# Edge constants per edge in their original order, and a hand-ordered beginning, in a four-layer graph network kernel

## The chip, the cores and the metric

The kernel runs on one core of one Trainium2 chip. The metric is the device time of one execution in microseconds (us). The kernel before took 3554.51 us, the median of three runs from 3550.32 to 3556.36.

The engines are TensorE (PE, matrix products; PEld is its weight load), VectorE (DVE), ScalarE (ACT), GpSimd (POOL) and SyncE (SP, which here only issues transfers). Transfers are issued on SP's, ACT's and POOL's queues and are carried out by 16 DMA engines that all queues share.

## What is computed

The input `x` holds 128 graphs of 128 nodes with 256 features, `adj` is one 128 x 128 matrix for all, and there are 512 edges `src`, `dst`. Four layers follow, each as `x = layernorm(x + layer(x))`. Layer 0 is an attention over edges:

```
Xq, Xv = H @ W_lin.T, H @ W_val.T               # 4 heads of 64
e = einsum(leaky_relu(Xq[:, src] + Xq[:, dst], 0.2), a)
e = e + log(adj[src, dst] + 1e-8)
e_t = e.transpose(1, 0, 2)                      # edges first
m = segment_max(e_t, src);  ex = exp(e_t - m[src])
attn = ex / segment_sum(ex, src)[src]
Y = segment_sum(attn * Xv[:, dst], src)         # back to graph, node, feature
out = Y @ W_out.T
```

Layer 1 is three rounds of `adj^2 @ (h @ W)` with relu between them, layer 2 three products with the diagonal, the upper and the lower part of `adj`, and layer 3 a normalized adjacency product, two dense layers and two batch norms over all graphs.

## The kernel before

The graphs are worked in 32 quads of four. The main loop, `iteration(k)` for k from 0 to 32, is a software pipeline with the order of instructions written out by hand: it works layer 2 and the first half of layer 3 on quad k-1, the large products of layer 1 (`second`, line 325, and `third`, line 336) on quad k, the end of layer 0 and the start of layer 1 on quad k+1 (`stage_a`, `mix1`, `first`, `mix2`), the scores and the softmax of layer 0 on quad k+2, and the projection to `Xq` and `Xv` with its gather on quad k+3 (`values_in`, `values`, `gather`). PE runs through the list in order; so does every other engine and every queue. A second phase after the loop finishes layer 3.

One quad's path through layer 0 has these steps:

- `values_in` (lines 145 to 157) loads a quad of `x` to the single buffer `xg` on SP's queue, transposes it on PE (line 154) and copies it to `xt` (line 156). `values` (line 159 on) multiplies it with `wqv` (line 167), copies one half to `qt` on ACT (line 168) and the other to `xv` on DVE (line 169), and after the fourth graph writes `qt` to `qd` in DRAM (line 172).
- `gather` (line 174 on) fetches four tiles of 128 edges from `qd` with eight indirect transfers on POOL (line 180): by `src_idx`, then by `dst_idx`, which adds to what the first brought.
- `score` (line 184 on) does leaky relu, the product with `a` and a sum over 64 for each of the four tiles, three DVE instructions over 128 x 1024 (lines 190, 192 and 193).
- `softmax_parts` transposes the scores on PE (line 200), adds the edges' logarithms `log_row` (line 202) and does maximum and sum by segment as scans along the edges, which are sorted by source (lines 205, 208, 214 and 216), with Exp on ACT (line 212). It is a generator; the caller steps it between other work.
- `attention` transposes back (line 226) and divides (lines 228 and 230). `scatter` writes four tiles to the table `attd` in DRAM (line 236), each after the one before it has landed, and loads the table as `ad` on SP's queue (line 239). `by_row` re-arranges it on ACT (line 246). `stage_a` then aggregates (line 258), projects (line 270) and normalizes.

Ahead of the loop (lines 431 to 596 for the set-up and the loads, 655 to 688 for filling the pipeline) stands a beginning whose order the framework's scheduler chooses. It does quad 0's projection, the edge set-up, the adjacency set-up (`wt_t`, `split_t`, `diag_bc`, `ahat_t`), the loads of all weights, and then fills the pipeline: layer 0 up to `mix2` of quad 0, quad 1 up to its scatter, quad 2 up to its gather. The first instruction of the loop on PE is line 325 of `second(0)`.

The edge set-up sorts the edges by source with comparisons of 128 x 512 (`rank`, `perm`), turns sources and destinations into sorted columns and, broadcast over 128 partitions, sorted rows (`ends_ps`, line 489), and computes each edge's constants in the sorted order: how often the pair occurs (`count`, line 517), whether it occurred earlier (`again`, `earlier`, line 520), and `adj[src, dst]` through two one-hot products (lines 540 and 544). The logarithm is kept as a row of 16 x 512.

Of the kernel before, what the change touches and what calls it, by code (L numbers as in the profile page):

```python
# [17 lines left out]
LOG_EPS = 1e-8  # L18
# [6 lines left out]
def gnn_stack(ctx: ExitStack, tc: tile.TileContext, x, adj, w_qv_t, a, w_out_t, src, dst,  # L25
# [80 lines left out]
    with ExitStack() as phase:  # L106
# [14 lines left out]
        a_sb = cload([P, N], "adj", adj)  # L121
        xg0 = load_x(0, "xg", 1)
        wqv = cload([P, DC, 2 * D], "wqv", w_qv_t.rearrange("(c p) f -> p c f", p=P))
        a_bc = cload([P, D], "a_bc", bass.AP(tensor=a.tensor, offset=a.offset, ap=[[0, P], [1, D]]), nc.scalar)

# [7 lines left out]
        log_row = ctile([R, E], "log_row", pool=cst)  # L133
# [11 lines left out]
        def values_in(k, xg=None):  # L145

            s = quads[k]
            s.xts = []
            xg = load_x(k, "xg", 1) if xg is None else xg
            for j in range(0, QB, 2):  # L150
                pt = ps("pt").rearrange("p (b c n) -> p b c n", b=2, c=DC)
                for t in range(2):
                    for c in range(DC):
                        nc.tensor.transpose(pt[:, t, c, :], xg[:, j + t, c * P:(c + 1) * P], ident)  # L154
                xt = ws.tile([P, 2, DC, P], F32, tag="xt", name="xt")
                nc.vector.tensor_copy(xt, pt)  # L156
                s.xts.append(xt)

        def values(k, i):

            s = quads[k]
# [7 lines left out]
            nc.vector.tensor_copy(s.xv[:, i, :], pq[:, D:])  # L169
# [4 lines left out]
        def gather(k):  # L174

            s = quads[k]
            s.z = [ws.tile([P, QB * D], F32, tag="zs", name=f"zs{k}_{c}", bufs=NE) for c in range(NE)]
            for idx, op in ((src_idx, ALU.bypass), (dst_idx, ALU.add)):
                for c in range(NE):
                    nc.gpsimd.indirect_dma_start(out=s.z[c], out_offset=None, in_=s.qd,  # L180
                                                 in_offset=bass.IndirectOffsetOnAxis(ap=idx[:, c:c + 1], axis=0),
                                                 compute_op=op)

        def score(k, c):
# [8 lines left out]
            nc.vector.reduce_sum(s.es[:, c, :], z.rearrange("p (r d) -> p r d", d=DH), axis=AX.X)  # L193

        def softmax_parts(k):
# [5 lines left out]
            e = wk.tile([R, E], F32, tag="e", name="e", bufs=1)  # L201
            nc.vector.tensor_add(e, log_row, pe[:R, :])
            yield
            f = wk.tile([R, E], F32, tag="f", name="f", bufs=1)
            nc.vector.tensor_tensor_scan(f, reset_f, e, initial=0.0, op0=ALU.add, op1=ALU.max)
# [5 lines left out]
            nc.vector.tensor_sub(e, e, m)  # L211
# [217 lines left out]


        values_in(0, xg0)
        for i in range(QB):
            values(0, i)
        with tc.tile_pool(name="set", bufs=1) as sp:
            src_col = cload([P, NE], "src_col", src.rearrange("(c p) -> p c", p=P), nc.scalar, I32, sp)
            dst_col = cload([P, NE], "dst_col", dst.rearrange("(c p) -> p c", p=P), nc.scalar, I32, sp)
            src_row = cload([P, E], "src_row", bass.AP(tensor=src.tensor, offset=src.offset, ap=[[0, P], [1, E]]),
                            nc.scalar, I32, sp)
            ones = ctile([P, P], "ones", pool=sp)
            nc.vector.memset(ones, 1.0)  # L440
            zero = ctile([P, N * R], "zero", pool=sp)
            nc.gpsimd.memset(zero, 0.0)
            for ad in att_dram:
                nc.scalar.dma_start(ad[:N * N, :].rearrange("(t s) r -> t (s r)", s=N), zero)


            pos = ctile([P, E], "pos", pool=sp)
            nc.gpsimd.iota(pos, pattern=[[1, E]], base=0, channel_multiplier=0,
                           allow_small_or_imprecise_dtypes=True)
            pos_col = ctile([P, NE], "pos_col", pool=sp)  # L450
            nc.gpsimd.iota(pos_col, pattern=[[P, NE]], base=0, channel_multiplier=1,
                           allow_small_or_imprecise_dtypes=True)
            ends = ctile([P, 2, NE], "ends", pool=sp)
            nc.vector.tensor_copy(ends[:, 0, :], src_col)
            nc.vector.tensor_copy(ends[:, 1, :], dst_col)
            key_row = ctile([P, E], "key_row", pool=sp)
            nc.vector.tensor_copy(key_row, src_row)
            nc.vector.scalar_tensor_tensor(key_row, key_row, float(E), pos, op0=ALU.mult, op1=ALU.add)
            key_col = ctile([P, NE], "key_col", pool=sp)
            nc.vector.scalar_tensor_tensor(key_col, ends[:, 0, :], float(E), pos_col, op0=ALU.mult, op1=ALU.add)  # L460

            less = ctile([P, NE, E], "less", pool=sp)
            rank = ctile([P, NE], "rank", pool=sp)
            perm = ctile([P, NE, E], "perm", pool=sp)
            bcast = ctile([P, 2, NE, P], "bcast", pool=sp)
            for c in range(NE):
                nc.vector.tensor_scalar(less[:, c, :], key_row, key_col[:, c:c + 1], None, op0=ALU.is_lt)
            nc.vector.reduce_sum(rank, less, axis=AX.X)
            for c in range(NE):
                nc.vector.tensor_scalar(perm[:, c, :], pos, rank[:, c:c + 1], None, op0=ALU.is_equal)  # L470
                for t in range(2):
                    nc.vector.tensor_copy(bcast[:, t, c, :], ends[:, t, c:c + 1].to_broadcast([P, P]))


            pc = ps("pcol")[:, :NE * 2].rearrange("p (c t) -> p c t", t=2)
            for c in range(NE):
                for i in range(NE):
                    nc.tensor.matmul(pc[:, c, :], perm[:, i, c * P:(c + 1) * P], ends[:, :, i],
                                     start=(i == 0), stop=(i == NE - 1))
            cols = ctile([P, NE, 2], "cols", pool=sp)  # L480
            nc.vector.tensor_copy(cols, pc)
            nc.vector.tensor_copy(src_idx, cols[:, :, 0])
            nc.vector.tensor_copy(dst_idx, cols[:, :, 1])

            ends_row = ctile([P, 2, E], "ends_row", pool=sp)
            for t in range(2):
                pr = ps("ends_ps")
                for c in range(NE):
                    nc.tensor.matmul(pr, bcast[:, t, c, :], perm[:, c, :], start=(c == 0), stop=(c == NE - 1))
                nc.vector.tensor_copy(ends_row[:, t, :], pr)  # L490


            pair_row = ctile([P, E], "pair_row", pool=sp)
            nc.vector.scalar_tensor_tensor(pair_row, ends_row[:, 1, :], float(N), ends_row[:, 0, :],
                                           op0=ALU.mult, op1=ALU.add)
            pair_col = ctile([P, NE], "pair_col", pool=sp)
# [103 lines left out]
        def iteration(k):  # L600
            a, c, b, e, g = k - 1, k, k + 1, k + 2, k + 3
            has_a, has_c, has_b, has_e, has_g = a >= 0, c < NQ, b < NQ, e < NQ, g < NQ
            if has_b:
                quads[b].xr = load_x(b, "xr", 3, wk)
# [200 lines left out]
```

## Time and profile before

| | |
|---|---|
| median of three runs | 3554.51 us |
| the profiled execution's own time | 3562.3 us |
| its span, from the first instruction to the last | 3560.1 us |
| PE busy | 3370.1 us, 95% of the span |
| DVE busy | 1801.2 us, 51% |
| ACT busy | 1004.9 us, 28% |
| POOL busy | 542.1 us, 15% |
| mean DMA rate | 98 GB/s |

The profile is of one execution, and its times are for comparing parts with each other. A page of it shows the busy share of each engine in 40 slices of 89 us as digits in tenths. A row of a windows table gives, for a stretch, the busy time of each engine with the number of its instructions, PE's granted clock, the DMA engines' busy share and the rate in GB/s. A row of waits names an instruction, what released it, the idle time in total, how often, and the longest. A row of the timeline gives start, duration, engine, line, operation and tiles.

### The profile page before, as it was taken

The numbers are of one execution on the slowest core, as the hardware profiler recorded it, in microseconds if no ns is written. First come the engines' busy times: TensorE is split into PE (matmuls) and PEld (weight loads), VectorE is DVE, ScalarE is ACT, GpSimd is POOL, SyncE is SP. The second block draws the span as 40 slices with busy tenths as digits, with TensorE's granted clock in tenths as the row PEclk, the third lists the DMA queues.
The fourth block names the chain that finished last, engine by engine and source line by source line (L and its number), as shares of the span: only waits on it lengthen the run. The fifth ranks groups of instructions, "written<-read, shape, count | busy, mean of one in ns | idle before, by whom it ended". The sixth has DMA issues, their size and how long they took to land.

```text
span 3560.1 us, 32948 instructions
## 1 busy us (share of the span) xinstructions
PE 3370.1 (95%) x12618; PEld 2146.1 (60%) x12618; DVE 1801.2 (51%) x3645; ACT 1004.9 (28%) x1733; POOL 542.1 (15%) x460
## 2 busy tenths in 40 slices
PE   5599999999999999999999999999999999989963
PEld 2366666666666666666666666666666666654442
DVE  6544455545545445544455555545445543223379
ACT  1122222222222222222222222222222222224452
POOL 2211111111111111111111111111111110000000
PEclk7799999999999999999999999999999999999975
DMA  6433333333222333333333333222333330025447
GB/s 190 124 83 89 90 95 95 85 87 93 80 76 73 89 95 95 95 95 90 88 95 95 89 84 95 81 77 74 85 95 95 95 89 36 18 95 183 154 137 223
DMA packets 127741, 347.72 MB, mean 98 GB/s; under 512 B 14433, under 2 KB 68577, under 8 KB 115041
## 3 DMA queue, kind: packets, MB, share of 16 engines
q0 software_dynamic: 40960, 135.29, 15.9%
q1 hardware_dynamic: 65168, 190.53, 15.0%
q10 hardware_dynamic: 21456, 19.81, 1.7%
q8 instruction: 99, 1.62, 0.2%
q14 instruction: 58, 0.47, 0.0%
HBM read 258.55 MB, written 87.03 MB: 97 GB/s over the span
## 4 chain that ended last, share of the span: by engine, by line
PE 88%; DVE 6%; DMA 2%; issue 1%; ACT 1%; POOL 0%; DVEq 0%; POOLq 0%; ACTq 0%; SPq 0%
PE ph L325 25%; PE p L336 13%; PE po L384 9%; PE po L739 6%; PE ph L423 6%; PE ph L305 6%; PE pq L167 6%; PE pm L315 3%; PE pm L370 3%; PE po L270 3%; PE py L258 2%; PE pa L409 2%; PE pm L291 2%; PE po L347 2%; DVE x3l L98 1%
## 5 line engine op out<-in xcount | busy, mean ns | idle before, releaser
L325 PE MATMUL ph<-m,w 128*128 128x512 f32 x2048 | 885.9, 593 | 2.7 <-DVE m L316 2.7
L325 PEld LDWEIGHTS ph<-m,w 128*128 128x128 f32 x2048 | 389.6, 190 | 480.1 <-issue 475.6
L336 PE MATMUL p<-w,h 128*128 128x256 f32 x2048 | 450.4, 381 | 0.0
L336 PEld LDWEIGHTS p<-w,h 128*128 128x128 f32 x2048 | 386.6, 190 | 52.6 <-issue 0.5
L180 POOL DMA_INDIRECT zs<-qd,src_idx x128 | 126.7, 989 | 1846.2 <-DVE f L214 1676.1
L384 PE MATMUL po<-l2w,ms 128*128 128x256 f32 x1536 | 347.5, 379 | 1.2 <-DVE ms L376 1.2
L328 ACT ACTIVATE h<-ph 128x512 f32<-128x512 f32 x256 | 153.2, 598 | 595.6 <-PE ph L325 595.6
L384 PEld LDWEIGHTS po<-l2w,ms 128*128 128x128 f32 x1536 | 284.3, 190 | 36.1 <-DVE ms L376 1.4
L305 PE MATMUL ph<-w,mx 128*128 128x512 f32 x512 | 236.3, 594 | 0.0
L167 PE MATMUL pq<-wqv,xt 128*128 128x512 f32 x512 | 232.0, 607 | 2.9 <-DVE xt L156 2.9
L739 PE MATMUL po<-zl,l3w 128*128 128x512 f32 x512 | 222.1, 597 | 10.4 <-ACT zl L734 10.4
L423 PE MATMUL ph<-ag,l3w 128*128 128x512 f32 x512 | 226.5, 595 | 0.4 <-ACT ag L412 0.4
L180 POOL DMA_INDIRECT zs<-qd,dst_idx x128 | 200.4, 1566 | 117.8 <-DMA zs<-qd,src_idx 95.5
L349 DVE TENSOR_TENSOR xr<-xr,po 128x512 f32<-128x512 f32 x64 | 43.8, 684 | 340.5 <-PE po L347 340.5
L156 DVE COPY xt<-pt 128x512 f32<-128x512 f32 x64 | 41.4, 686 | 309.5 <-PE pt L154 309.5
L236 POOL DMA_INDIRECT attd<-at,att_idx x128 | 127.9, 999 | 439.9 <-DMA attd<-at,att_idx 282.7
L90 ACT ACTIVATE ln_sd<-ln_mv,eps 128x2 f32<-128x2 f32 x256 | 75.8, 296 | 379.2 <-DVE ln_mv L85 374.1
L739 PEld LDWEIGHTS po<-zl,l3w 128*128 128x128 f32 x512 | 98.0, 192 | 134.5 <-issue 111.1
L190 DVE SCALAR_TENSOR_TENSOR zs<-zs 128x1024 f32<-128x1024 f32 x128 | 155.7, 1217 | 33.1 <-DMA zs<-qd,dst_idx 33.1
L423 PEld LDWEIGHTS ph<-ag,l3w 128*128 128x128 f32 x512 | 97.4, 191 | 122.3 <-issue 113.0
L167 PEld LDWEIGHTS pq<-wqv,xt 128*128 128x128 f32 x512 | 97.4, 195 | 115.8 <-issue 111.4
L316 DVE COPY m<-pm 128x512 f32<-128x512 f32 x128 | 88.4, 692 | 153.8 <-PE pm L315 153.8
(173 smaller groups left out, 4237.8 us busy)
## 6 DMA issues: line engine op xcount, KB each, us to landing
ad<-attd SPq DMA_DIRECT2D x32, 1024.0 KB, 4.7
zd<-z SPq DMA_DIRECT2D x32, 1024.0 KB, 7.4
zl<-zd SPq DMA_DIRECT2D x32, 1024.0 KB, 4.7
xg<-in_x_dram SPq DMA_DIRECT2D x32, 512.0 KB, 4.2
qd<-qt SPq DMA_DIRECT2D x32, 512.0 KB, 2.6
xr<-in_x_dram SPq DMA_DIRECT2D x32, 512.0 KB, 5.7
x3d<-xr SPq DMA_DIRECT2D x32, 512.0 KB, 2.9
x3l<-x3d SPq DMA_DIRECT2D x32, 512.0 KB, 4.2
```

Of the source, the lines that this page charges most:

```text
L167: nc.tensor.matmul(pq, s.xts[i // 2][:, i % 2, c, :], wqv[:, c, :], start=(c == 0), stop=(c == DC - 1))
L180: nc.gpsimd.indirect_dma_start(out=s.z[c], out_offset=None, in_=s.qd, in_offset=bass.IndirectOffsetOnAxis(ap=idx[:, c:c + 1], axis=0), com ...
L190: nc.vector.scalar_tensor_tensor(z, z, SLOPE, z, op0=ALU.mult, op1=ALU.max)
L236: nc.gpsimd.indirect_dma_start(out=ad, out_offset=bass.IndirectOffsetOnAxis(ap=att_idx[:, c:c + 1], axis=0), in_=s.at[:, c, :], in_offset= ...
L270: nc.tensor.matmul(po[:, i % 2, :], yts[i][:, dc, :], wo[:, dc, :], start=(dc == 0), stop=(dc == DC - 1))
L305: nc.tensor.matmul(ph, s.mx[i // 2 * 2][:, i % 2, dc, :], w1_sb[:, dc, :], start=(dc == 0), stop=(dc == DC - 1))
L325: nc.tensor.matmul(ph, w2_sb[:, c, f * P:(f + 1) * P], s.m2[:, c].rearrange("p b n -> p (b n)"), start=(c == 0), stop=(c == K1 - 1))
L328: nc.scalar.activation(h.rearrange("p b n -> p (b n)"), ph, AF.Relu)
L336: nc.tensor.matmul(p3[:, t * D:(t + 1) * D], s.h2[f][:, j + t, :], w3_sb[:, f, :], start=(f == 0), stop=(f == K2 - 1))
L384: nc.tensor.matmul(po[:, i % 2, :], mss[i][:, t, dc, :], l2w[:, t, dc, :], start=(n3 == 0), stop=(n3 == 3 * DC - 1))
L423: nc.tensor.matmul(ph, l3w1[:, dc, c * P:(c + 1) * P], s.ag[:, dc, :], start=(dc == 0), stop=(dc == DC - 1))
L739: nc.tensor.matmul(po, w2t[:, c, o * P:(o + 1) * P], z[:, c, :], start=(c == 0), stop=(c == K3 - 1))
```

## The change

The edge constants are computed per edge in the original order, as columns of 128 x 4: the comparisons add up their own result with an accumulated output, `adj[src, dst]` is fetched with four indirect transfers of 4 bytes for each edge, and the finished constants are brought to the sorted order with the same permutation product that sorts the ends (`sorted_columns`, called twice). The logarithm becomes a column `log_col`, which `score` adds to the scores before they are transposed; the add of `log_row` in `softmax_parts` goes away, and its scan and its subtraction read the transposed scores from PSUM.

The whole beginning becomes a function `start()` inside the hand-ordered part. In it, copies of `values_in` and `values` for quads 0 to 2 are on ACT; quad 0's gather has an interleaved order; the weights, the zero fill of `attd` and quad 0's `xr` are issued on SP's queue after quad 1's `qd`; quad 1's gather uses other tiles (`z`, `xb`, `ag`), and its scores stand after quad 0's scatter; the adjacency set-up stands between quad 0's scatter and quad 1's scores; quad 0's `stage_a` stands ahead of the last score and the softmax of quad 1; and quad 3's `values_in` and `values` are done there, with iteration 0 leaving them out. In the loop the softmax steps stand after the second and fourth product of `values` rather than after the first three. The diff, cut to its core:

```diff
-        a_sb = cload([P, N], "adj", adj)
         xg0 = load_x(0, "xg", 1)
         wqv = cload([P, DC, 2 * D], "wqv", w_qv_t.rearrange("(c p) f -> p c f", p=P))
-        a_bc = cload([P, D], "a_bc", bass.AP(tensor=a.tensor, offset=a.offset, ap=[[0, P], [1, D]]), nc.scalar)
-
+        a_sb = cload([P, N], "adj", adj)
+        a_bc = ctile([P, D], "a_bc", pool=cst)
...
-        def values_in(k, xg=None):
+        def values_in(k, xg=None, copy=None):
...
-                nc.vector.tensor_copy(xt, pt)
+                copy(xt, pt)
...
-            nc.vector.tensor_copy(s.xv[:, i, :], pq[:, D:])
+            copy(s.xv[:, i, :], pq[:, D:])
...
+            s.z = z or [ws.tile([P, QB * D], F32, tag="zs", name=f"zs{k}_{c}", bufs=NE) for c in range(NE)]
+            jobs = [(t, c) for t in range(2) for c in range(NE)]
+            if k == 0:
+                jobs = [(0, 0), (0, 1), (1, 0), (0, 2), (1, 1), (0, 3), (1, 2), (1, 3)]
+            for t, c in jobs:
+                idx, op = ((src_idx, ALU.bypass), (dst_idx, ALU.add))[t]
+                nc.gpsimd.indirect_dma_start(out=s.z[c], out_offset=None, in_=s.qd,
+                                             in_offset=bass.IndirectOffsetOnAxis(ap=idx[:, c:c + 1], axis=0),
...
+            if c == NE - 1:
+                nc.vector.tensor_add(s.es, s.es, log_col.unsqueeze(2).to_broadcast([P, NE, R]))
...
-            e = wk.tile([R, E], F32, tag="e", name="e", bufs=1)
-            nc.vector.tensor_add(e, log_row, pe[:R, :])
-            yield
             f = wk.tile([R, E], F32, tag="f", name="f", bufs=1)
-            nc.vector.tensor_tensor_scan(f, reset_f, e, initial=0.0, op0=ALU.add, op1=ALU.max)
...
-            nc.vector.tensor_sub(e, e, m)
+            e = wk.tile([R, E], F32, tag="e", name="e", bufs=1)
+            nc.vector.tensor_sub(e, pe[:R, :], m)
...
-        values_in(0, xg0)
-        for i in range(QB):
-            values(0, i)
-        with tc.tile_pool(name="set", bufs=1) as sp:
...
-            for c in range(NE):
-                nc.vector.tensor_scalar(less[:, c, :], key_row, key_col[:, c:c + 1], None, op0=ALU.is_lt)
-            nc.vector.reduce_sum(rank, less, axis=AX.X)
...
-            for ad in att_dram:
-                nc.scalar.dma_start(ad[:N * N, :].rearrange("(t s) r -> t (s r)", s=N), zero)
...
-            ends_row = ctile([P, 2, E], "ends_row", pool=sp)
-            for t in range(2):
-                pr = ps("ends_ps")
-                for c in range(NE):
-                    nc.tensor.matmul(pr, bcast[:, t, c, :], perm[:, c, :], start=(c == 0), stop=(c == NE - 1))
-                nc.vector.tensor_copy(ends_row[:, t, :], pr)
...
-            count = ps("count")
-            for c in range(NE):
-                nc.tensor.matmul(count, ones, same[:, c, :], start=(c == 0), stop=(c == NE - 1))
-            earlier = ps("earlier")
-            for c in range(NE):
-                nc.tensor.matmul(earlier, ones, less[:, c, :], start=(c == 0), stop=(c == NE - 1))
...
-            pr = ps("adj_e")
-            nc.tensor.matmul(pr, a_sb, g_src, start=True, stop=True)
-            picked = ctile([P, E], "picked", pool=sp)
-            nc.vector.tensor_mul(picked, g_dst, pr)
-            pr = ps("adj_e2")
...
-        gather(0)
-        edges(0)
-        whole(1)
-        attention(0)
-        scatter(0)
-        gather(1)
-        edges(1)
-        attention(1)
-        whole(2)
...
+            first_one = k == 0
...
-            if has_g:
+            if has_g and not first_one:
                 values_in(g)
...
-                if has_g:
+                if has_g and not first_one:
                     values(g, i)
-                if i < 3:
+                if i in (1, 3):
                     next(steps, None)
...
+        def start():
+            cols_i = wk.tile([P, 2, NE], I32, tag="cols_i", name="cols_i", bufs=1)
+            rows_i = [scratch(f"row_i{t}", I32) for t in range(2)]
+            for t, ap in ((0, src), (1, dst)):
+                nc.scalar.dma_start(cols_i[:, t, :], ap.rearrange("(c p) -> p c", p=P))
+            for t, ap in ((0, src), (1, dst)):
+                nc.scalar.dma_start(rows_i[t], bass.AP(tensor=ap.tensor, offset=ap.offset, ap=[[0, P], [1, E]]))
+            nc.scalar.dma_start(a_bc, bass.AP(tensor=a.tensor, offset=a.offset, ap=[[0, P], [1, D]]))
...
+            less = scratch("less")
+            for c in range(NE):
+                nc.vector.tensor_scalar(less, key_row, key_col[:, c:c + 1], 0.0, op0=ALU.is_lt, op1=ALU.add,
+                                        accum_out=rank[:, c:c + 1])
+            perm = wk.tile([P, NE, E], F32, tag="m2", name="perm", bufs=1)
+            for c in range(NE):
+                nc.vector.tensor_scalar(perm[:, c, :], pos, rank[:, c:c + 1], None, op0=ALU.is_equal)
...
+            for c in range(NE):
+                nc.gpsimd.indirect_dma_start(out=picked[:, c:c + 1], out_offset=None,
+                                             in_=adj.rearrange("n (m o) -> (n m) o", o=1),
+                                             in_offset=bass.IndirectOffsetOnAxis(ap=adj_idx[:, c:c + 1], axis=0))
+            values_in(0, xg0, nc.scalar.copy)
+            for i in range(QB):
+                values(0, i, nc.scalar.copy)
+            pc = sorted_columns(0)
+            nc.vector.tensor_copy(src_idx, pc[:, :, 0])
+            nc.vector.tensor_copy(dst_idx, pc[:, :, 1])
+            gather(0)
+            pr = ps("src_row")
+            for c in range(NE):
+                nc.tensor.matmul(pr[:R, :], src_wide[:, c, :], perm[:, c, :], start=(c == 0), stop=(c == NE - 1))
+            src_row = scratch("src_row")
+            nc.scalar.copy(src_row[:R, :], pr[:R, :])
...
+            same = scratch("same")
+            for c in range(NE):
+                nc.vector.tensor_scalar(same, pair_row, pair_col[:, c:c + 1], 0.0, op0=ALU.is_equal, op1=ALU.add,
+                                        accum_out=count[:, c:c + 1])
+                nc.vector.scalar_tensor_tensor(same, pos, pos_col[:, c:c + 1], same, op0=ALU.is_lt, op1=ALU.mult,
+                                               accum_out=again[:, c:c + 1])
...
+            nc.vector.scalar_tensor_tensor(weight, picked, LOG_EPS, count, op0=ALU.add, op1=ALU.mult)
+            nc.scalar.activation(weight, weight, AF.Ln)
+            nc.vector.scalar_tensor_tensor(ends[:, 3, :], again, DROP, weight, op0=ALU.mult, op1=ALU.add)
...
+            values_in(1, copy=nc.scalar.copy)
+            pc = sorted_columns(2)
+            nc.vector.tensor_copy(att_idx, pc[:, :, 0])
+            nc.vector.tensor_copy(log_col, pc[:, :, 1])
+            for i in range(QB):
+                values(1, i, nc.scalar.copy)
...
+            nc.sync.dma_start(wo, w_out_t.rearrange("(c p) f -> p c f", p=P))
+            nc.sync.dma_start(w1_sb, w1.rearrange("(c p) f -> p c f", p=P))
+            for ad in att_dram:
+                nc.sync.dma_start(ad[:N * N, :].rearrange("(t s) r -> t (s r)", s=N), zero)
+            quads[0].xr = load_x(0, "xr", 3, wk)
+            nc.sync.dma_start(w2_sb, w2.rearrange("(c p) f -> p c f", p=P))
+            nc.sync.dma_start(w3_sb, w3.rearrange("(c p) f -> p c f", p=P))
+            nc.sync.dma_start(l2w, l2_w.rearrange("k (c p) f -> p k c f", p=P))
+            nc.sync.dma_start(bias, bass.AP(tensor=l2_bias.tensor, offset=l2_bias.offset, ap=[[0, P], [1, D]]))
+            nc.sync.dma_start(l3w1, l3_w1_t.rearrange("(c p) f -> p c f", p=P))
+            for c in range(NE):
+                score(0, c)
+            z2 = wk.tile([P, 2, QB * D], F32, tag="z", name="z_1", bufs=1)
+            gather(1, [z2[:, 0, :], z2[:, 1, :], wk.tile([P, QB * D], F32, tag="xb", name="xb_1", bufs=1),
+                       wk.tile([P, QB * D], F32, tag="ag", name="ag_1", bufs=1)])
+            xg2 = load_x(2, "xg", 1)
+            steps = softmax_parts(0)
+            for _ in range(2):
+                next(steps)
+            values_in(2, xg2, nc.scalar.copy)
+            next(steps)
+            values(2, 0, nc.scalar.copy)
+            values(2, 1, nc.scalar.copy)
+            for _ in steps:
+                pass
+            attention(0)
+            for i in (2, 3):
+                values(2, i, nc.scalar.copy)
+            xg3 = load_x(3, "xg", 1)
+            scatter(0)
+            gather(2)
...
+            for c in range(NE - 1):
+                score(1, c)
+            for j in range(QB):
+                by_row(0, j)
+            stage_a(0)
+            score(1, NE - 1)
+            values_in(3, xg3)
+            steps = softmax_parts(1)
+            for i in range(QB):
+                next(steps)
+                values(3, i)
+            for _ in steps:
+                pass
+            attention(1)
+            scatter(1)
+            mix1(0, 0)
+            mix1(0, 2)
+            first(0, 0)
+            for i in range(QB):
+                if i + 1 < QB:
+                    first(0, i + 1)
+                mix2(0, i)
...
         with tc.manual_schedule(engines=None):
+            start()
             for k in range(NQ + 1):
                 iteration(k)
```

## The prediction

> **What bounds the kernel now.** I read the slices of the page first.
>
> ```profile
> span 3560.1 us, 32948 instructions
> ...
> PE   5599999999999999999999999999999999989963
> ...
> PEclk7799999999999999999999999999999999999975
> ```
>
> TensorE (PE) is full from slice 3 on; only the first two slices of 89 us and the last three are not. The diff touches the first two. Stage by stage:
>
> ```profile
> core 0: us, PE busy (x) PEld busy (x) DVE busy (x) ACT busy (x) POOL busy (x), PEclk, DMA share, GB/s
> 0.00:162.77 162.77, 84.97 (x267) 47.74 (x267) 94.89 (x164) 22.57 (x37) 44.99 (x44) 0.74 0.60 172
> 162.77:300.00 137.23, 134.68 (x462) 80.33 (x463) 63.64 (x108) 37.82 (x64) 18.73 (x17) 0.98 0.22 60
> ...
> 1000.00:2000.00 1000.00, 998.04 (x3852) 647.57 (x3851) 507.50 (x947) 276.05 (x479) 167.95 (x140) 1.00 0.30 86
> ```
>
> Before 162.77 us, where the first L325 matmul (`second(0)`) starts, PE is idle for 162.77 - 84.97 = 77.8 us. In the loop it is idle 2 us in 1000. So the whole question is when `second(0)` starts, and what of iteration 0 is done ahead of it. The waits of that stretch name the holes:
>
> ```profile
> PE pe L200 <- DVE es L193: 46.1, 6, 33.0
> PE half_ps L586 <- DVE half L584: 8.2, 1, 8.2
> PE pt L154 <- DMA xg<-in_x_dram: 7.3, 1, 7.3
> ```
>
> The 33.0 us are quad 1's scores waiting for a gather that shared the DMA engines with weights, scatter and attention table. SyncE's (SP's) queue in the timeline shows when they were issued:
>
> ```profile
> 58.19 0.37 SPq L111 DMA_DIRECT2D wo<-in_w_out_t_dram  x1
> 58.61 1.53 SPq L111 DMA_DIRECT2D w<-in_w_dram  x3
> 60.18 4.31 SPq L111 DMA_DIRECT2D l2w<-in_l_w_dram  x1
> 64.52 2.05 SPq L111 DMA_DIRECT2D bias<-in_l_bias_dram  x1
> 66.61 0.82 SPq L111 DMA_DIRECT2D l3w<-in_l_w_t_dram  x1
> ...
> 76.47 0.38 SPq L118 DMA_DIRECT2D xg<-in_x_dram  x1
> ```
>
> The rates, in windows of 5 us (columns as above):
>
> ```profile
> 60.00:65.00 5.00, 0.48 (x2) 0.18 (x2) 5.00 (x6) 0.00 (x0) 0.00 (x0) 0.50 1.04 410
> ...
> 95.00:100.00 5.00, 0.00 (x0) 0.00 (x0) 0.00 (x0) 0.00 (x0) 4.09 (x4) 0.50 0.83 162
> ```
>
> Weights alone move 410 GB/s. Beside an accumulating gather all traffic together makes 162.
>
> **What the Trainium skill says.** "DMA: Bandwidth & Descriptors", Queues, rings and completion order: on each DMA engine the descriptors of one queue are consumed in ring order; so a small load behind 8 MB on SP's queue comes last. Same page, SWDGE vs HWDGE vs iDMA: an engine goes round-robin between GpSimd's (POOL's) queue and the others. The trace agrees: the 1 MB load of `ad`, issued at 96.25 beside the gather of quad 1, landed at 105.15, 8.9 us, where the median over the page is 4.7. "TensorE: Matmul & The Clock Gate", What's actually happening: an idle PE falls to half clock. The trace has 0.50 from 80 to 120 us.
>
> **The change, part by part.** Times are of the profiled execution (span 3560.1, its own time 3562.3); I apply the difference to the median 3554.5, 7.8 below it.
>
> (1) Set-up, removed: 16 matmuls of `ends_ps` (9.43 us), the `count` and `earlier` ones (9.1), `adj_e` (2.1): 20.6 us of PE, plus DVE's reduces of 2048 (2.29 + 2.27), four `less` products, the row forms. Added: 8 matmuls for `src_row` (4.7 by `ends_ps`), a second `pcol` set (4.66), four 4-byte gathers of `adj` at 1.25 us of POOL each, if a small one costs what a 4 KB row does (hidden: adj_idx is there at about 9, so they end at 14, and `qd` lands only at 21; uncovered they would be 5 us). Accumulating forms of `less`, `same`, `again` aren't in the trace: at least the plain 0.42 and 0.66 us, at most double; I take 0.65 and 0.75. The spread is 12 x 0.4 = under 5 us, and most sits in (2), beside other work.
>
> (2) Quad 0 to gather(0). The copies of `xt` and `xv` go to ACT, which is idle. PE's first pq no longer waits for DVE (2.7): start 8.4 instead of 11.93, last `qt` at 18.4 instead of 21.9. The input of quad 1 is now behind this `qd` on SP's queue: issued at 18.8, there at 23.4 (4.6 to landing), and PE wants it after `src_row`, at 27.4: hidden. `pcol` 4.7, two casts: gather(0) starts at 23, not 26.9. Its new order makes dst 0 wait for src 0; z 0 lands by 39 at worst (dst issue to use was 7.5 at 145.5), and DVE is busy until then anyway: free.
>
> (3) Quad 1. DVE from 23: pair keys 0.85, four same/again pairs 6, small ones and Ln 1.6: 31.5. PE: second `pcol` to 36.3, then values(1) at 8.4 (as at 126.9): 44.7. Last `qt`, `qd` issued at 45. `pcol` waits at the head of PE's queue, but only values(1) is behind it.
>
> (4) Quad 0's scores: keep/reset to 38.5, then 4 x 3.74 (153.06 to 156.8) and the new 128x64 add at 0.2 (as L230): 53.7. Transposes, two scans, subtract: 57.5.
>
> (5) The new wait. SP's queue now holds `wo`, `w1`, the two 1 MB zero fills (until now on ACT's queue at the very start), `xr`, `w2`, `w3`, `l2w`, `bias`, `l3w` all behind `qd` of quad 1, and the `xg` of quad 2 behind them: 8.5 MB from 45. Behind this `xg` stand, on PE, pt and half of pq of quad 2 and then attention(0)'s pat; on ACT, two `xt` copies and then quad 0's Exp. So quad 0's softmax stops at 57.5 until quad 2's input is there. At the rate of the old weights (5.25 MB in 58.2 to 74.5, 322 GB/s) that is 26.5 us: 71. Gather(1) runs beside it: 2 MB at 386 GB/s (the window of 5 to 10 us) and 2 MB at 199 (35 to 40 us, accumulating) are some 15 us more of the same engines: 87 if all of it comes out of SP's share. I take 80; both ends go into the range.
>
> (6) From 80: transposes and copies 2.7, table load and Exp 1.9, two scans 2.5, pat, reciprocal, multiply 1.3: `at` at 88.4. Four scatters in a row, 10.3 (128.21 to the `ad` issue at 138.47): 98.7. `ad` load 4.7 to 8.9, I take 7, since gather(2) starts with it: 105.7; first by_row copy 106.8. The adjacency set-up, hidden before, now sits between attention(0) and score(1, 0 to 2): PE after the rest of pq at 92, its handshakes with DVE and a table load about 5, then 3 x 3.74: DVE is free at 108. So it costs 1 us here, on the path.
>
> (7) stage_a 10.5 (136.5 to 147.0): 118.5. score(1, 3) with the add 3.9: 122.4. Copies of `xt`, then softmax woven with values(3) 11.7 (192.7 to 204.3, less the dropped L202): 134.1. pat and mix1 to mix2: 0.8 and 17 (145.01 to 162.77 less 0.7 of wait): **second(0) at 152**, 10.8 earlier.
>
> (8) Iteration 0 drops values_in(3) and values(3). Before, from the end of second (192.0) to the first stage_a projection (204.84) 12.8 us passed. Now PE has only pe and py there, and waits for the softmax chain: 0.6 + two scans 2.4, 0.7, Exp 0.6, two scans 2.4, first `yt` 0.4, gaps 0.6: 7.7. Gain 5.1, not the 8 us of matmuls, since softmax is late next.
>
> (9) The loop. Per iteration DVE loses L202 (0.67) and gains an add (0.2). PE is full (2 us idle in 1000): zero. At most its idle 6 us are gained; a loss would need DVE, half idle, to come late. Nothing in the tail changes.
>
> Sum: -10.8 - 5.1 = -15.9. Profiled 3546.4; against the median **3538.6**.
>
> **Rivals.** A: the loads hardly hinder. POOL's gathers wait for each other and leave gaps, SP's queue runs at 322 GB/s, `xg` is there at 71 and `ad` in 4.7: -9 - 2 more, total -27, 3527.6. For it: from 60 to 70 us the same queue drew 382 to 410 GB/s, so an unhindered stretch is worth much. Against it: 95 to 100 us, where two kinds of traffic together moved less than one alone. B: scatter and `ad` run loaded, as quad 0's did at 78.16 to 96.25 (18.1 instead of 10.3) and 8.9: +9.7, total -6.2, 3548. Against it: SP's queue is empty by then; only gather(2) comes after. C, slower: SP's queue behind gather(1) gets the 162 GB/s of the window at 95, all of it shared. Then 8.5 MB take over 50 us. From 80 on everything hangs on `xg` one for one, so the gain is gone at 80 + 15.9 = 96; at 106 the time is +10, 3564.5. Against it: that gather can't be busy for 50 us, it has 15 us of engine time.
>
> **How the numbers follow.** Forecast 0.57 (its own range 3531 to 3546), A 0.17, B 0.17, C 0.09. About 0.2%, 7.1 us, is what a measurement can tell from no change. Forecast and A are beyond it (0.74), a quarter of B too: faster 0.78, same 0.13, slower 0.09. The range leaves out C and the edge of A: 3522 to 3552.
>
> **What would show it.** In the profile after: gather(0) near 23 us; `qd` of quad 1 near 45 and the weights right behind; ACT's quad-2 `xt` copies near 80 with `xg` as releaser, DVE idle from about 57 to 84; `at` near 88, adc near 107, the first L329 near 152; in iteration 0 a PE wait of about 5 us for `yt`. Wrong would be: `xg` of quad 2 long before 70 or after 95, PE waiting elsewhere (for scores of quad 1), or a loop whose PE idle differs from 2 us in 1000.

## The result, and the profile after

| | before | after |
|---|---|---|
| median | 3555.44 us (4 runs, 3550.32 to 3562.93) | 3565.62 us (4 runs, 3564.43 to 3566.78) |
| profiled execution: own time, span | 3562.3, 3560.1 us | 3564.83, 3562.8 us |
| `second(0)` starts | 162.77 us | 174.23 us |
| from there to the last `second` | 2964.33 us | 2957.47 us |
| from there to the end | 433.00 us | 431.10 us |

The ratio after to before is 1.0027, 95% interval 1.0008 to 1.0046: slower by 0.3%, where 3538.6 us and a gain were forecast. The profiled execution of the kernel before lies at the top of its runs, so the spans differ by only 2.7 us and the medians by 10.2. In three later sets of 19 to 27 runs the kernel before had medians of 3557.98 to 3561.12; against those the loss would be 4.5 to 7.6 us.

PE's slices on the page of after, and two rows of its windows table with the columns of the prediction:

```profile
PE   4599999999999999999999999999999999989963
```

```profile
0.00:174.23 174.23, 83.16 (x295) 49.35 (x295) 74.04 (x137) 30.52 (x60) 49.35 (x47) 0.73 0.54 158
174.23:3131.70 2957.47, 2945.12 (x11356) 1914.03 (x11357) 1465.85 (x2778) 809.13 (x1412) 519.14 (x414) 1.00 0.29 85
```

The picture is that of before: the loss is ahead of `second(0)`. DVE has 20.9 us less to do there (74.04 against 94.89) and PE 1.8 less, yet the stretch is 11.5 us longer: for these two the start has more idle time, not more work. The waits of after up to 174.23 name it (releaser, total, times, longest):

```profile
PE pt L154 <- DMA xg<-in_x_dram: 39.3, 2, 34.1
DVE f L218 <- ACT e L216: 35.5, 1, 35.5
...
ACT sums L660 <- DVE sums L659: 21.0, 1, 21.0
...
PE col_ps L657 <- DVE adj_t L651: 20.5, 1, 20.5
DVE adj_t L651 <- POOL split_t L643: 19.7, 1, 19.7
```

The first two rows are the wait for quad 2's `xg` that step (5) forecast. The last three are in no step: DVE waits 19.7 us for POOL in the adjacency set-up, and ACT and PE wait behind it. SP's queue in the timeline of after gives the first two their cause (start, duration, as before):

```profile
41.69 0.33 SPq L173 DMA_DIRECT2D qd<-qt  x1
...
51.71 16.82 SPq L609 DMA_DIRECT2D l2w<-in_l_w_dram  x1
68.57 6.13 SPq L610 DMA_DIRECT2D bias<-in_l_bias_dram  x1
74.74 0.55 SPq L611 DMA_DIRECT2D l3w<-in_l_w_t_dram  x1
75.38 0.99 SPq L118 DMA_DIRECT2D xg<-in_x_dram  x1
```

SP is still issuing weights when DVE runs dry at 53.7, and gets to `xg` at 75.38; PE has it at 84.58. POOL's and DVE's timelines of after show the other wait (the bracket is the idle time before an instruction and what ended it):

```profile
93.92 1.02 POOL L240 DMA_INDIRECT attd<-at,att_idx  x1 [30.33 <-DVE at L234]
...
103.96 1.00 POOL L184 DMA_INDIRECT zs<-qd,src_idx  x1 [0.30 <-issue]
...
115.91 1.53 POOL L184 DMA_INDIRECT zs<-qd,dst_idx  x1 [0.30 <-issue]
116.87 0.89 POOL L641 TENSOR_SCALAR_AFFINE_SELECT split_t<-adj_t 128x128 f32<-128x128 f32 x1
117.12 0.89 POOL L643 TENSOR_SCALAR_AFFINE_SELECT split_t<-adj_t 128x128 f32<-128x128 f32 x1
```

```profile
98.03 0.29 DVE L649 COPY diag_bc<-diag_ps 128x128 f32<-128x128 f32 x1 [0.64 <-PE diag_ps L648]
118.04 0.29 DVE L651 TENSOR_TENSOR adj_t<-adj,ident 128x128 f32<-128x128 f32 x1 [19.72 <-POOL split_t L643]
...
121.07 1.22 DVE L194 SCALAR_TENSOR_TENSOR z<-z 128x1024 f32<-128x1024 f32 x1
...
132.13 0.77 DVE L266 COPY yt<-py 64x256 f32<-64x256 f32 x2
```

In `start()` the line before L651 is `an = adj_t`, where the kernel before gives `an` a tile of its own (its line 569): L651 writes its sum over the tile that the two affine selects on POOL still have to read. The selects were issued behind `scatter(0)` and `gather(2)`, twelve transfers in POOL's queue. Two operations of under a microsecond so hold up DVE, and behind L651 in DVE's queue stand three scores of quad 1 and, behind those, DVE's first `yt` of `stage_a`. ACT is held too: `ad` landed at 110.8, but its copy by ACT (L250) stands behind the square root of L660, which needs L651's result, and starts at 119.56. The Trainium skill has the rule, in "PSUM — Partial Sum Buffer", Engine vs sequencer instructions: the queues of DVE, ACT and POOL are strictly first in, first out. The trace agrees: no instruction of either queue passed its head.

### The profile page after: what moved, and what is told of

Its sections match the earlier page's. It is cut to its first block, busy times and chain, and to the rows that moved or that the text cites. A ratio compares the mean times of both kernels' runs of the same rounds, so it can differ in the third digit from the quotient of the medians.

```text
span 3562.8 us, 32962 instructions
## 1 busy us (share of the span) xinstructions
PE 3358.6 (94%) x12622; PEld 2144.3 (60%) x12622; DVE 1782.8 (50%) x3618; ACT 1008.7 (28%) x1751; POOL 571.0 (16%) x463
## 4 chain that ended last, share of the span: by engine, by line
PE 89%; DVE 6%; DMA 2%; ACT 1%; SPq 1%; issue 1%; POOL 0%; DVEq 0%; ACTq 0%; POOLq 0%
PE ph L329 25%; PE p L340 13%; PE po L388 9%; PE po L743 6%; PE ph L309 6%; PE pq L168 6%; PE ph L427 6%; PE pm L319 3%; PE pm L374 3%; PE po L274 3%; PE py L262 2%; PE pm L295 2%; PE pa L413 2%; PE po L351 2%; DVE x3l L98 1%; DVE x3l L762 1%
## 5 line engine op out<-in xcount | busy, mean ns | idle before, releaser
L184 POOL DMA_INDIRECT zs<-qd,src_idx x124 | 148.9, 1201 | 1763.0 <-DMA qd<-qt 1654.8
L320 DVE COPY m<-pm 128x512 f32<-128x512 f32 x128 | 88.5, 691 | 152.8 <-PE pm L319 152.8
L319 PEld LDWEIGHTS pm<-wt_t,h 128*128 128x128 f32 x1024 | 131.8, 191 | 47.7 <-issue 40.2
```

The source lines that it names most:

```text
L319: nc.tensor.matmul(pm[:, c, :], s.h1[i][:, c * P:(c + 1) * P], wt_t, start=True, stop=True)
```

## The experiments

Theory: two waits in `start()` eat the gain, the reuse of `adj_t` (about 19 us) and `xg` of quad 2 behind the weights, and the rest of the change does what it was priced at. Rival: the start is bound by `ad` and the DMA traffic, and with one wait gone the next is close behind. Edits are against the kernel after unless said otherwise; ratios are to the kernel before, run beside them (medians 3557.98 for e1 to e4, 3559.97 for e5 to e8, 3561.12 for e9 and e10). The three sets ran on three different chips, and the kernel after was in none of them, so a difference of medians across sets, or to after, is less certain than a ratio by up to the 5.7 us between the medians of before.

| kernel | median us | ratio, 95% interval | `second(0)` |
|---|---|---|---|
| e1_own_an | 3546.77 | 0.9962, 0.9949 to 0.9976 | 158.59 |
| e2_gather2_late | 3551.82 | 0.9981, 0.9972 to 0.9989 | 159.43 |
| e3_xg2_first | 3553.57 | 0.9986, 0.9978 to 0.9993 | 162.30 |
| e4_both | 3532.22 | 0.9921, 0.9907 to 0.9934 | 139.46 |
| e5_weights_late | 3525.64 | 0.9904, 0.9890 to 0.9918 | 137.90 |
| e6_values3_loop | 3551.73 | 0.9978, 0.9970 to 0.9986 | 154.44 |
| e7_constants | 3558.20 | 1.0001, 0.9992 to 1.0009 | 156.64 |
| e8_auto | 3528.93 | 0.9913, 0.9900 to 0.9926 | 137.06 |
| e9_rest_early | 3519.36 | 0.9887, 0.9873 to 0.9901 | 128.45 |
| e10_constants_set | 3560.40 | 0.9999, 0.9990 to 1.0007 | 159.46 |

**e1: the reused tile.**

```diff
-            an = adj_t
+            an = wk.tile([P, N], F32, tag="an", name="an", bufs=1)
```

> Base: the changed kernel, 3565.6 us. Edit: `an` gets a tile of its own instead of the tile of adj_t. Theory W (write after read): the add of L651 waits 19.7 us on VectorE for the two affine selects, which stand behind gather(2) on GpSimd; all of stage_a(0) hangs on it. Then L651 runs at 98.3, ahat_t is done at 101, three scores at 112.5, ad has landed at 110.8, so the first yt is at 113 instead of 132.1, and second(0) starts 19 us earlier, near 155: 3546.6 us. Rival Q (SP's queue: the late xg of quad 2 alone makes the start late, and the 20 us only overlap a wait for ad and by_row that would be there anyway): no more than 2 us, 3564. Rival L (the loop became slower): no change of the start matters beyond its own size, and PE is idle more than 2 us in 1000 in the loop.

Measured 3546.77, 18.9 us under after. DVE's timeline of e1:

```profile
98.05 0.29 DVE L649 COPY diag_bc<-diag_ps 128x128 f32<-128x128 f32 x1 [0.64 <-PE diag_ps L648]
98.26 0.28 DVE L651 TENSOR_TENSOR an<-adj,ident 128x128 f32<-128x128 f32 x1
...
101.17 1.22 DVE L194 SCALAR_TENSOR_TENSOR z<-z 128x1024 f32<-128x1024 f32 x1
```

The wait is gone, with nothing else moved up to there, and the sign of the whole change turns. Of DVE's 19.8 us, 15.6 arrive at `second(0)`: now the load of `ad` is late next, 12.2 us of ACT's wait at L250, as the rival says. (PE, which needs ACT's copies, starts `stage_a` at 113.06.)

**e2: the same wait shortened from the other side.** The tile stays shared; `gather(2)` leaves the place ahead of the selects.

```diff
             scatter(0)
-            gather(2)
...
             nc.vector.tensor_scalar(ahat_t, pr, dinv, None, op0=ALU.mult)
+            gather(2)
```

> Base: the changed kernel, 3565.6 us. Edit: gather(2) is issued after the adjacency set-up instead of before it; `an` still shares the tile of adj_t. Theory W: the selects now stand right behind scatter(0), whose last issue ended at 103.7, so L651 runs near 105 instead of 118 and everything after it is 13 us earlier: 3552.6 us. If the shared tile were costly in itself and not the place of the selects on GpSimd, no change. Rival Q: no more than 2 us, 3564.

3551.82. The same add (L650 here) starts right after the fourth scatter and the two selects, and not at 118.0:

```profile
103.21 0.29 DVE L650 TENSOR_TENSOR adj_t<-adj,ident 128x128 f32<-128x128 f32 x1 [5.93 <-POOL split_t L642]
```

It still waits 5.9 us of the 19.7. So it is what stands ahead of the selects in POOL's queue, and not the selects themselves, that makes the wait. `second(0)` starts only 0.8 us after that of e1; why e2's median is 5 us above e1's isn't shown.

**e3 and e4: quad 2's input ahead of the weights,** with the shared tile (e3) and with its own (e4).

```diff
+            xg2 = load_x(2, "xg", 1)
             nc.sync.dma_start(wo, w_out_t.rearrange("(c p) f -> p c f", p=P))
...
-            xg2 = load_x(2, "xg", 1)
```

> Base: the changed kernel, 3565.6 us. Edit: the load of quad 2's xg is issued ahead of the weights on SP's queue. Theory W with the late input as a second wait: Exp of quad 0 near 55 instead of 88.5, `at` near 60, the scatter then runs under the load of the weights (18 instead of 10 us) and behind gather(1), gather(2) waits for its qd behind the weights, and L651 still waits for gather(2) on GpSimd: near 98 instead of 118, so 20 us earlier, 3545.6 us. Rival Q: the whole 34 us of waiting for xg comes off, 3531 us. If only the shared tile matters and the input is hidden by it: no more than 5 us, 3561.

> Base: the changed kernel, 3565.6 us. Edit: both, `an` in its own tile and quad 2's xg ahead of the weights. Theory W with two waits in a row: `at` near 60, the adjacency set-up done near 67, scores of quad 1 when its gather has landed, to 84, scatter(0) under load to 83, ad near 90, first yt near 92 instead of 132.1: 40 us earlier, 3525.6 us. Rival: the chain scatter, ad, by_row under the load of weights is so slow that this gains no more than the better of the single edits, about 3545.

e3 gave 3553.57, 8.0 us short of the expectation, e4 3532.22, 6.6 short. Exp of quad 0 moved from 88.5 to 54.2, but the waits of e3 and then of e4 show what took its place:

```profile
DVE adj_t L651 <- POOL split_t L643: 39.0, 1, 39.0
```

```profile
ACT adc L250 <- DMA ad<-attd: 30.6, 1, 30.6
```

The first scatter, which after lets the next one go after 2.4 us (93.92 to 96.35), now takes 13 (64.55 to 77.71 in e3): it meets the weights and quad 1's accumulating gather. With the shared tile DVE waits 39.0 us, since the selects stand behind these scatters and `gather(2)`. The own tile is worth 18.9 us without the early load and 21.4 with it; the early load 12.1 and 14.6. So there are two separate waits: taking away both brings 33.4 us, a little more than the 30.9 of the single edits together.

**e5: the five late weights out of the way,** e4 with `w2`, `w3`, `l2w`, `bias` and `l3w1` issued behind the scatters' `ad`.

```diff
-            nc.sync.dma_start(w2_sb, w2.rearrange("(c p) f -> p c f", p=P))
...
             scatter(0)
             gather(2)
+            nc.sync.dma_start(w2_sb, w2.rearrange("(c p) f -> p c f", p=P))
...
```

> Base: the kernel with both edits (own tile for `an`, quad 2's xg first), 3532.2 us, in which second(0) starts at 139.5. Edit: w2, w3, l2w, bias and l3w1 (4.6 MB) are issued behind the load of ad instead of ahead of it. There the first scatter took 13 us to land and the four together with ad went from 64.4 to 95.1. Theory W with a third wait in the same row (scatter, ad and gather(1) share the DMA engines with weights that second(0) wants 40 us later): the scatters end near 78, ad lands near 84, first yt near 88 instead of 99.3, 11 us earlier: 3521 us. Rival: the first scatter is slow because the accumulating gather of quad 1 is ahead of it in GpSimd's own queue, and weights don't matter: no more than 3 us, 3530.

3525.64, 6.6 us under e4 by medians but only 1.6 at `second(0)`. The profiled executions are e5's slowest run and e4's fastest, and e5's has quad 1's `qd` 3.6 us later (last section). POOL's timeline of e5:

```profile
65.78 1.53 POOL L184 DMA_INDIRECT ag<-qd,dst_idx  x1 [0.30 <-issue]
67.61 1.02 POOL L240 DMA_INDIRECT attd<-at,att_idx  x1 [0.30 <-DVE sums L662]
77.78 1.62 POOL L240 DMA_INDIRECT attd<-at,att_idx  x1 [9.15 <-DMA attd<-at,att_idx]
```

The first scatter still takes 10.2 us with those weights not yet issued. What the DMA engines carried from its issue to 75 us shows why (packets, MB, share of the engines' time, summing to a little over 100%; q0 carries POOL's transfers, q1 SP's):

```profile
q0 software_dynamic: 305, 1.12, 75.8%
q1 hardware_dynamic: 400, 0.79, 30.2%
```

Up to then q0 moves the rest of quad 1's gather. In the trace's records of single packets the scatter's 16 packets of 512 bytes start only at 75.6 us, 8.0 after the issue, among the last of the gather's 4 KB packets; in these 8.0 us the gather's packets took 6.1 us of the engines' time and SP's 2.3. In e4, with the weights, the same wait is 11.5 us, of which the gather took 8.6 and SP 3.5; in after, with no gather ahead, it is 1.6. So the rival has the cause: most of the lateness is the accumulating gather ahead of the scatter on POOL's own queue. My expectation of 3521 put too much on the weights.

**e6: values(3) back in iteration 0,** on top of e1.

```diff
-            first_one = k == 0
+            first_one = False
...
-            values_in(3, xg3)
...
-                values(3, i)
```

> Base: the kernel with `an` in its own tile, 3546.8 us. Edit: values_in(3) and values(3) go back to iteration 0, out of start(). If moving them gained what step (8) says: iteration 0 takes 5.3 us more between the end of second(0) and the first projection (12.8 instead of 7.5), and start() loses the part of values(3) that its softmax doesn't cover, 3.4 us (pe to pat 11.0 now, 7.6 for the softmax chain alone): 1.9 us slower, 3548.7. Rival: the move cost nothing in start() and is worth its 8 us of matmuls: 3554.

3551.73, 5.0 us over e1. `second(0)` starts 4.2 us earlier (154.44), but from there to the last `second` it takes 2963.0 us as in before (2964.3), where e1 takes 2957.4. So moving the work ahead gains 5.6 in the loop and costs 4.2 in the start; another 2.2 come after the last `second` (433.2 against 431.0 us), which I can't explain. That makes 3.6 us between the profiled spans; e1 and e6 ran in different sets, so the 5.0 of the medians is the less certain figure.

**e7 and e10: the edge constants alone,** with the scheduler's beginning of the kernel before. In e7 the set-up has no buffers of its own and the weights go out from 5 us on; in e10 they wait for the set-up's scratch buffers, as before.

```diff
-        with tc.manual_schedule(engines=None):
-            start()
+        values_in(0, xg0)
+        for i in range(QB):
+            values(0, i)
+        start()
+        gather(0)
+        edges(0)
+        whole(1)
...
```

> Base: the kernel before, 3555.4 us. One part of the change alone: the edge constants per edge in the original order, in the beginning of the kernel before, with its calls in their old order and the scheduler choosing (`an` in its own tile). The scheduler now places the weights' loads at the very start, since they no longer wait for the set-up's buffers; qd of quad 0 is behind them on SP's queue, so gather(0) starts near 29. Theory: the logarithms are ready near 35 instead of 50 and the weights are out of the way of gather(1), scatter and ad: quad 1's scores end near 104 instead of 118, second(0) starts near 149 instead of 163, 3541 us. Rival: the early weights hold qd of quad 0 up so long that nothing is gained, 3555.

> The edge constants in original order alone, in the beginning of the kernel before, with its scratch pool for set-up kept, so that the weights wait for the set-up's buffers again as they do in the kernel before. Theory (the constants save the second permutation of the edge fields, and what they save in the set-up reaches second(0)): set-up ends some 9 us earlier, the weights are issued at about 49 instead of 58, second(0) starts at about 155 instead of 162.8, time about 3550 us, ratio about 0.998. Rival (the set-up isn't on the path that sets second(0), or its gain is lost in the loads that now come sooner, as in the constants alone without the pool): no difference, 3557 us, ratio 1.000.

Both rivals held: ratios 1.0001 and 0.9999. The constants alone bring nothing that can be measured. In e7 the weights stand ahead of quad 0's `qd` (issued at 19.2, first gather 29.3 instead of 26.9). In e10 the weights still go out at 58.68 (58.19 before). Two lines of POOL's timeline of e10 show one place where the saving stays:

```profile
46.80 1.21 POOL L590 TENSOR_SCALAR_AFFINE_SELECT split_t<-adj_t 128x128 f32<-128x128 f32 x1 [12.64 <-DVE adj_t L588]
...
50.30 1.56 POOL L184 DMA_INDIRECT zs<-qd,dst_idx  x1 [0.30 <-issue]
```

The scheduler set the selects between quad 0's gathers, the last of which leaves at 50.3 us instead of 38.6; its last score ends at 64.3, before at 64.8. Again a small operation in POOL's queue waits for DVE, and what is behind it waits too.

**e8: the same program as after with the order of `start()` left to the scheduler.**

```diff
+        start()
         with tc.manual_schedule(engines=None):
-            start()
```

> Base: the changed kernel, 3565.6 us. Edit: start() is called just outside the hand-ordered part, so that the scheduler chooses the order of the very same instructions and tiles. It puts the weights at the start, the affine selects behind the first scatter, and L651 ahead of quad 1's second score. Theory W (the order on SP's and GpSimd's queues is what costs): both waits are gone though the tile is still shared, Exp of quad 0 near 56, scatter near 64 to 76, ad near 82, second(0) near 126 instead of 174: 3518 us. Rival (the time lies in what start() computes and not in its order): no more than 10 us, 3556.

3528.93: 36.7 us under after with not one operation changed, though 10.9 over the expectation (Exp of quad 0 runs at 62.75 instead of 56, `second(0)` starts at 137.06 instead of 126). The scheduler issues the weights from 5 us on, and in POOL's queue it puts the selects directly behind the first scatter instead of behind twelve transfers. Two rows of the timeline of e8:

```profile
73.56 0.34 POOL L643 TENSOR_SCALAR_AFFINE_SELECT split_t<-adj_t 128x128 f32<-128x128 f32 x1
...
74.90 0.28 DVE L651 TENSOR_TENSOR adj_t<-adj,ident 128x128 f32<-128x128 f32 x1
```

L651 runs at 74.9 instead of 118.0 and, with the tile still shared, has no wait of its own. It is the hand-written order, not the work in it, that makes after slow.

**e9: e5 with `wo`, `w1`, the zero fills and `xr` issued right behind quad 1's `xg`,** at 16 us.

```diff
+            xg1 = load_x(1, "xg", 1)
+            nc.sync.dma_start(wo, w_out_t.rearrange("(c p) f -> p c f", p=P))
...
+            quads[0].xr = load_x(0, "xr", 3, wk)
-            values_in(1, copy=nc.scalar.copy)
+            values_in(1, xg1, nc.scalar.copy)
```

> As the run with the late weights (3525.64 us), but wo, w1, the zero fills and the first residual load are issued right after the load of quad 1's xg, before quad 1's values, instead of behind quad 1's qd. Theory (quad 1's chain and the adjacency's gathers still wait for bytes ahead of them): what is left ahead of quad 2's xg is 1.3 MB less, the index values of quad 2 come about 3 us earlier, the adjacency with them, and the score of stage 3 too: second(0) starts at about 134 instead of 137.9, time about 3521 us, ratio to before about 0.989. Rival: the same bytes now share the rings with the accumulating gathers of quad 0, which come later by as much (first scores of quad 0 at 30 instead of 27), and the whole chain behind them with it: second(0) at 138 or later, 3526 us or more.

3519.36, the fastest: 46.3 us under after, ratio 0.9887 to before. The rival's mishap came too (quad 0's last score ends at 54.9 instead of 51.7), but quad 1's gather has the engines to itself and the scatter behind it is quick, as POOL's timeline of e9 shows:

```profile
59.20 1.53 POOL L184 DMA_INDIRECT ag<-qd,dst_idx  x1 [0.30 <-issue]
64.66 1.02 POOL L240 DMA_INDIRECT attd<-at,att_idx  x1 [3.92 <-DVE at L234]
69.24 1.01 POOL L240 DMA_INDIRECT attd<-at,att_idx  x1 [3.56 <-DMA attd<-at,att_idx]
```

`ad` is issued at 77.30 instead of 85.30. That is more than the 3 us expected; 3.9 of it is quad 1's `qd`, at 41.3 instead of 45.2, which is e5's slow stretch on PE (last section) as much as e9's merit, since e4 had it at 41.6.

## Why the prediction was wrong

Its order of events in the start holds up to step (5) and from step (8) on. The step that failed is **(6)**: "The adjacency set-up, hidden before, now sits between attention(0) and score(1, 0 to 2): PE after the rest of pq at 92, its handshakes with DVE and a table load about 5, then 3 x 3.74: DVE is free at 108. So it costs 1 us here, on the path." I counted the handshakes of PE, DVE and ACT and left POOL's selects out, though the same step has four scatters in POOL's queue and `gather(2)` behind them, and the added line `an = adj_t` that ties DVE to them. DVE was free at 132.1. Of the prediction's own signs of being wrong one came true: PE waited elsewhere, 20.5 us at L657, though for L651 and not for scores of quad 1.

- (1) The accumulating compares took 0.75 us plus 0.08 to read the sum (0.65 and 0.75 taken); the add for `log_col` 0.22. Right in size.
- (2), (3), (4) gather(0) at 19.1 (forecast 23), quad 1's `qd` at 41.7 (45), DVE dry at 53.7 (57.5): each some 4 us early, and all of it lost in the wait that follows.
- (5) The new wait was right: `xg` to PE at 84.58, in the bounds of 71 to 87, 4.6 later than the value taken. But the loads took longer than taken: SP's 8.5 MB took 42.9 us (41.7 to 84.6), against 35 taken (45 to 80) and 42 at the most, and the early start hid part of that. From 60 to 80 us all queues together moved 293 GB/s, less than the 322 taken for SP's alone. The 386 GB/s taken for the plain half of the gather is from a window of direct loads; alone it moved 305 (50 to 56 us of e9).
- (6) `at` at 93.6 (forecast 88.4: the 4.6, and 0.6 more), `ad` issued at 104.8 and landed at 110.8 (98.7 and 105.7). Then the missed wait: DVE's first `yt` of `stage_a` at 132.1 instead of 108. In e1 it comes at 116.2, so 16 us of these 24 are the reused tile; of the other 8, 5 are the late `at`, and 3 lie between the first by_row copy and this `yt` (4.2 us in e1, 1.2 in the forecast).
- (7) `stage_a` 13.3 instead of 10.5 (10.3 in e1; PE's granted clock in after was 0.50 from 130 to 135 us and 0.66 from 135 to 140), score 3.9 as forecast, softmax with values(3) 11.1 (11.7), the rest to `second(0)` 13.8 (17.8). Together 24.1 + 2.8 - 0.6 - 4.0 = 22.3 us: from the forecast 152 to 174.2.
- (8) Iteration 0 gained 5.3 us (7.5 instead of 12.8 from the end of `second` to the first projection; forecast 5.1). PE's waits of after between 201 and 212 us, with the forecast wait of about 5 us for `yt`:

```profile
PE po L274 <- DVE yt L266: 5.1, 1, 5.1
```

- (9) The loop: PE busy 2693.39 us from 300 to 3000, before 2692.76. Zero, as forecast.

The sum in spans: forecast -15.9, plus 22.3 of the start, minus 1.8 more in the loop (1.7 of it `second(0)` itself, at a granted clock of 1.00 instead of 0.94) and 1.9 in the tail, makes 2.7, the measured difference. By medians the miss is larger, 27.0 us instead of 18.6. The other 8.4 come from a second mis-sized term, "I apply the difference to the median 3554.5, 7.8 below it": the profiled execution of after lay not 7.8 above its median but 0.8 below it.

With the one missed wait taken out the forecast holds as a ratio: it was 3538.6 to 3554.51, 0.9955, and e1 ran at 0.9962, 0.9949 to 0.9976. Part of that is luck: e1's `second(0)` starts at 158.59, 6.6 us after the forecast 152, while loop and tail brought 3.8 more than forecast.

Rival C named 3564.5 us, one off the measured time, but by another way: it has `xg` at 106, and it came at 84.6. Rival A had it at 71, and rival B a loaded scatter of 18.1 us, which took 10.9. A number that fits is no proof of its mechanism; the wait in DVE's queue is.

What stays open: why e10 and e7, whose `second(0)` starts 3 to 6 us before that of the profiled before, are no faster in their medians. Their runs and those of before spread over some 12 us (3550 to 3564) while e4's and e9's lie within 3, so one profiled execution does not place their start well. The tail after the last `second`, the same code in after and all ten runs, took 431.0 to 433.4 us, and what moves it is not known.

## What to carry to other kernels

When a step is moved, list for each of its instructions the engine, what stands ahead of it in that engine's queue at the new place, and which later instruction writes a tile that it reads: a reused scratch tile cost no wait in e8, where its readers ran at once, and 19.7 us of DVE's time in after, where they sat behind a dozen transfers. An order by hand is worth checking against the scheduler's own order of the same program: here that alone was 36.7 us. And loads that nobody needs soon go where no accumulating gather or scatter is in flight, rather than simply late or early.

## What the runs showed of the hardware

- On POOL's queue the first scatter's bytes moved only behind those of the gather ahead of it. From its issue to its first packet passed 1.6 us with nothing ahead (after), 2.4 behind the rest of an accumulating gather (e9), 8.0 behind more of one beside 0.8 MB of SP's (e5), 11.5 beside 1.3 MB (e4). The next scatter followed after 2.4, 4.6, 10.2 and 13.2 us.
- Alone on the DMA engines, busy over 0.9 of the time, a plain gather of 4 KB rows moved 305 GB/s (50 to 56 us of e9), an accumulating one 201 (57 to 67 us).
- SP itself can be held up: issuing the 768 KB of `l2w` took it 4.3 to 5.9 us in the four kernels where no gather of a quad was in flight (before, e7, e8, e10), and 13.2 to 16.9 in after and the seven where one was. The bytes ahead of it on SP's queue don't order these: 3.8 MB in before, 4.1 in e5 with its 13.8 us, 6.4 in after. The trace doesn't show why.
- The same program can have two speeds on PE. Up to quad 1's `values` after and e1 to e6 are alike. In after, e2, e3 and e4 PE waits 2.6 us for `ends`, takes 5.2 over 32 products for `pcol`, and `qd` of quad 1 is issued at 41.6 to 41.7 us; in e1, e5 and e6 it waits 4.3, takes 7.0, and `qd` goes at 43.7 to 45.2. PE's granted clock from 30 to 40 us was 0.70 to 0.71 in the first group and 0.50 to 0.62 in the second. That the longer wait lowers the clock is not shown.
